# Filling the first image's idle matmul time, splitting weight stores over two queues, and pruning by weight rows: a convolution and attention kernel

## The chip, the cores and the metric

The kernel runs on one core of a Trainium2 chip. The metric is the device time of one execution, in microseconds (us). Five engines work beside each other, each in its own order: TensorE (PE in the profile, with its weight loads as PEld) multiplies matrices, VectorE (DVE) and ScalarE (ACT) work on tiles elementwise and reduce them, GpSimd (POOL) does some elementwise work, and SyncE (SP) starts DMA transfers. ScalarE can start transfers too. Engines wait for each other through semaphores. Matmul results arrive in PSUM and are read from there by VectorE or ScalarE.

## The reference, cut to what matters

Eight images of 512 channels and 32 x 32 pixels, in float32. Layer 0 is a residual block of a 1x1 convolution, two blocks of 3x3 convolution and attention, and a last 1x1 convolution over the four pieces; layer 1 is a depthwise and a pointwise convolution, with pruning of channels.

```python
# layer 0
t = cbs(x, cv1_w, cv1_bn, 0)              # cbs: convolution, batch norm, silu
ys = [t[:, :C], t[:, C:]]                 # C = 256
for i in range(2):
    yi = ys[-1]
    z = cbs(yi, m_cv1_w[i], m_cv1_bn[i], 1)            # 3x3
    z = bot_attention(z, m_qkv_w[i], m_rw[i], m_rh[i]) # 4 heads of 64, 1024 positions
    z = jax.nn.silu(bn_eval(conv2d(z, m_cv2_w[i], 0), m_cv2_bn[i]))
    ys.append(yi + z)
return cbs(jnp.concatenate(ys, axis=1), cv2_w, cv2_bn, 0)   # "the last convolution"

# layer 1
def _prune(x, thresh):
    amax = jnp.max(jnp.abs(x), axis=(2, 3), keepdims=True)
    return jnp.where(amax < thresh, jnp.zeros_like(x), x)
h = depthwise 3x3 of h, + dw_b
h = jax.nn.relu(_bn(h, ...))
h = _prune(h, 4.0)
h = pointwise 512 -> 512 of h, + pw_b
h = jax.nn.relu(_bn(h, ...))
h = _prune(h, 1e-3)

# both
x = x + layer0(_gn(x))     # _gn: group norm, 32 groups
x = x + layer1(_gn(x))
```

## The kernel before

Channels lie on the 128 partitions; an image is four tiles of 128 x 1024. Each engine keeps the order in which the program names its instructions (except GpSimd, which may be reordered), so this order decides what waits behind what. Background work is kept in lists of small functions that are "pumped" between others.

The 3x3 convolutions are computed in a transformed domain (a Winograd form). Their weights are transformed on the chip while the first image runs, written to DRAM (`u_dram`), and fetched from there for every image through a ring of four buffers. `along`, `inside` and `outside` are the steps for three pairs j of planes:

```python
    def transform_weights(l):
        ...
        def store(j, c, t):
            for m in range(2):
                src = t.rearrange("p (i m x) -> p i m x", i=2, m=2)[:, :, m]
                dst = u_dram[l][2 * j + m][:, :, c].rearrange("p i k o -> p i (k o)")
                nc.sync.dma_start(dst, src)
        def inner_rows(j, step): ...      # VectorE: "ucomp" tiles, stored
        def outer_rows(j, c, dy):         # ScalarE: "uplane" tiles, stored
            t = planes.pop((j, dy))
            nc.scalar.mul(t, t, 2.0)
            store(j, c, t)

    def ring_sources():                   # the order of all weight fetches
        for b in range(B):
            for l in range(2):
                for i in range(6):
                    yield u_dram[l][i]..., 2048
                yield wqkv[:, l]..., 1536
            for m in range(KC):
                yield w2[:, :, m * P : (m + 1) * P], 1024
    held = [len(sources) - 7, 0]          # fetches after these 7 are held until u1 is stored
```

The start of the program, for the first image:

```python
            fold = fold_norms()           # batch norm scales; GpSimd takes a power
            gn = [group_norm(pt, lambda c: pt[c], chunks) for chunks in ((0, 1), (2, 3))]
            ...
            pump(gn[1], 2)
            next(fold)
            flush(gn[1])
            next(fold)                    # waits for the power, then six small operations
            pump(first, 2)                # matmuls of the first convolution
            along, inside, outside = transform_weights(0)
            flush(along[0]); flush(along[2]); flush(inside[0]); flush(outside[0])
            ring_load(2)
            flush(first)
            flush(along[1]); flush(inside[1]); flush(outside[1])
            ring_load(2)
            flush(inside[2])
            pump(y0_work, 2)
            flush(outside[2])
            flush(y0_work)
            conv3(0, [], 0, [])
            ...
            qkv(0, ...)
            attention(taps, range(1, 20), lambda: None, [then])
            load(pt, 1)
```

The attention's end. `tail` is work for TensorE while the sums of the softmax are inverted, spread by DMA and multiplied into z; with `lambda: None` there is none:

```python
        parts, spread, check = sums(1)    # ps_dn on TensorE; ScalarE reads, VectorE inverts
        for part in parts:
            part()
        spread()                          # DMA: rw <- r
        tail()
        scale(1, 0)                       # VectorE: z = z * rw
        scale(1, 1)
        check()                           # ScalarE
```

What follows for every image (`halves` and `finishes` are work left from the image before, so they are empty in the first):

```python
        pump(finishes)
        cv2m(0)                           # ps_m: needs z
        pump(halves)
        conv3(1, halves, 1, finishes)     # ps_c: needs VectorE's transform of yp
        ...
        qkv(1, [], (0,) * 7)
        products, finish = cv2()          # the last convolution
        attention(stats[:KC], (6, 10, 14, 17), lambda: products(0, range(6)))
        stats = stats[KC:]
        cv2m(1)
        ...
        products(1, (0, 1, 2, 3))
        pump(stats)
        products(1, (4, 5))
        pump(stats)
        products(0, (6, 7))
        finish(0)                         # silu, then added to xt[0]
        ...                               # products(1, (6, 7)), finish(1), statistics, ...
```

`products(m, ks)` does the matmuls of output chunk m for the input chunks ks (0 and 1 are y0, 2 and 3 the first block's input, 4 and 5 its output, 6 and 7 the second block's output), two matmuls of 512 columns for each. Group norm's small steps:

```python
        def deviations():
            pv = ...                      # TensorE: group variance
            nc.vector.tensor_scalar(rs, pv[:, :n], 1e-5, None, ALU.add)
            nc.gpsimd.tensor_tensor(rs, rs, mhalf[:, :n], ALU.pow)
            nc.vector.scalar_tensor_tensor(nb, gm, -1.0, rs, ALU.mult, ALU.mult)
        def apply(i, c):
            nc.scalar.activation(dst(c), src[c], AF.Identity, bias=nb[...], scale=rs[...])
```

In the last image nothing of a next image is there to fill TensorE, and layer 1 is done with an order of its own. `taps(n)` are n of the 32 steps of the depthwise convolution on VectorE (eight for each chunk), `part(k, ...)` the pointwise products of input chunk k, `close(m)` relu and `finish(m)`:

```python
        def prune(c):
            keep = small.tile([P, 1], ...)
            nc.vector.tensor_reduce(keep, ht[c], AX.X, ALU.max)
            nc.vector.tensor_scalar(keep, keep, 4.0, None, ALU.is_ge)
            if c == KC - 1 and len(groups) == KC:
                w = wpw_sb[:, c, :]
                nc.vector.tensor_scalar(w, w, keep, None, ALU.mult)
            else:
                nc.gpsimd.tensor_scalar(ht[c], ht[c], keep, 1.0, ALU.mult, ALU.mult)

        def finish(m):
            w = box.pop(m)
            nc.vector.tensor_reduce(keep, w, AX.X, ALU.max)
            nc.vector.tensor_scalar(keep, keep, 1e-3, None, ALU.is_ge)
            nc.vector.scalar_tensor_tensor(xt[m], w, keep, xt[m], ALU.mult, ALU.add)
            nc.sync.dma_start(out[b, m * P : (m + 1) * P, :], xt[m])
    ...
    taps(3); relu(2); taps(2); prune(2); taps(6)
    part(2, every)
    relu(3); prune(3)
    for m in range(KC):
        part(3, [(m, 0), (m, 1)])
        close(m)
```

Of the kernel before, what the change touches and what calls it, by code (L numbers as in the profile page):

```python
# [1 line left out]

# [59 lines left out]
def fast_kernel(  # L62
# [174 lines left out]
    def transform_weights(l):  # L237
# [26 lines left out]
        def store(j, c, t):  # L264

            for m in range(2):
                src = t.rearrange("p (i m x) -> p i m x", i=2, m=2)[:, :, m]
                dst = u_dram[l][2 * j + m][:, :, c].rearrange("p i k o -> p i (k o)")
                nc.sync.dma_start(dst, src)
# [16 lines left out]
        def outer_rows(j, c, dy):  # L286
            t = planes.pop((j, dy))
            nc.scalar.mul(t, t, 2.0)
            store(j, c, t)
# [11 lines left out]
    def ring_sources():  # L301
        for b in range(B):
            for l in range(2):
                for i in range(6):
                    yield u_dram[l][i].rearrange("p a b c d -> p (a b c d)"), 2048
                yield wqkv[:, l].rearrange("p k o -> p (k o)"), 1536
            for m in range(KC):
                yield w2[:, :, m * P : (m + 1) * P], 1024
# [4 lines left out]
    held = [len(sources) - 7, 0]  # L313
# [14 lines left out]
    class Weights:  # L328
# [5 lines left out]
        def __exit__(self, *_):  # L334
            ring_load()

    def group_norm(src, dst, chunks):
# [24 lines left out]
        def deviations():  # L362
# [4 lines left out]
            nc.vector.scalar_tensor_tensor(nb, gm, -1.0, rs, ALU.mult, ALU.mult)  # L367

        def apply(i, c):
            nc.scalar.activation(  # L370
# [8 lines left out]
    def layer1_front(groups):  # L379
# [27 lines left out]
        def prune(c):  # L407
# [3 lines left out]
            if c == KC - 1 and len(groups) == KC:  # L411

                w = wpw_sb[:, c, :]
                nc.vector.tensor_scalar(w, w, keep, None, ALU.mult)
            else:
                nc.gpsimd.tensor_scalar(ht[c], ht[c], keep, 1.0, ALU.mult, ALU.mult)  # L416

        if len(groups) == KC:
# [12 lines left out]
    def layer1_back(b):  # L431
# [18 lines left out]
        def finish(m):  # L450
            w = box.pop(m)
            keep = small.tile([P, 1], F32, tag="keep2", name="keep2")
            nc.vector.tensor_reduce(keep, w, AX.X, ALU.max)
            nc.vector.tensor_scalar(keep, keep, 1e-3, None, ALU.is_ge)
# [417 lines left out]
    def cv2():  # L872
# [10 lines left out]
        def products(m, ks, ns=range(2)):  # L883
            if m not in open_:
                open_[m] = big_tile("ps_cv2"), ring.pop(0)
            ps, wt = open_[m]
            w = wt[:, : 2 * KC * P].rearrange("p (k o) -> p k o", o=P)
            for k in ks:
                for n in ns:
                    nc.tensor.matmul(  # L890
                        ps[:, n, :],
                        w[:, k, :],
                        rhs(k, n),
                        start=(k == 0),
                        stop=(k == 2 * KC - 1),
                    )

        def finish(m, pieces=1):
            ps, _ = open_.pop(m)
            ring_load()  # L900
            t = work_tile("c2")
            n, r = HW // pieces, 4 // pieces
            for q in range(pieces):
                act(t[:, q * n : (q + 1) * n], flat(ps)[:, q * n : (q + 1) * n], AF.Silu, BN1 + m)

                o = xt[m].rearrange("p (h t r) -> p h t r", t=F // 4, r=4)
                i = t.rearrange("p (r h t) -> p h t r", h=F, t=F // 4)
                o, i = (a[:, :, :, q * r : (q + 1) * r] for a in (o, i))
                nc.vector.tensor_tensor(o, i, o, ALU.add)

        return products, finish


    QUIET = (5, 8, 11, 14, 17, 18, 24, 26, 27, 28, 29, 30)
    halves, finishes, taps, before, late = [], [], [], [], []
    for b in range(B):
        if b:
# [9 lines left out]
            pump(late)  # L927
            pump(before, 2)
# [5 lines left out]
        else:  # L934
# [10 lines left out]
            flush(gn[1])  # L945
            next(fold)
            pump(first, 2)
            along, inside, outside = transform_weights(0)
            flush(along[0])
# [7 lines left out]
            flush(outside[1])  # L957
            ring_load(2)
            flush(inside[2])
            pump(y0_work, 2)  # L960
            flush(outside[2])
# [4 lines left out]
            along, inside, outside = transform_weights(1)  # L966
# [9 lines left out]
            attention(taps, range(1, 20), lambda: None, [then])  # L976
# [4 lines left out]
        cv2m(0)  # L981
        pump(halves)
# [4 lines left out]
        products, finish = cv2()  # L987
        attention(stats[:KC], (6, 10, 14, 17), lambda: products(0, range(6)))
# [5 lines left out]
        products(1, (0, 1, 2, 3))  # L994
        pump(stats)
        products(1, (4, 5))
        pump(stats)
        products(0, (6, 7))
# [53 lines left out]
    taps(2)  # L1052
# [6 lines left out]
    pump(gn[1])  # L1059
    before(1)  # L1060
# [496 lines left out]
```

## Time and profile before

| | us |
|---|---|
| time, median of 3 runs | 2702.61 (2702.23 to 2703.11) |
| profiled span | 2700.4, mean granted TensorE clock 0.992 |
| TensorE matmuls busy | 2631.7 (97%) |
| VectorE busy | 1978.2 (73%) |
| ScalarE busy | 1139.0 (42%) |
| GpSimd busy | 158.1 (6%) |
| DMA | 219.75 MB, mean 81 GB/s |

The page gives each engine's busy time, then the span in 40 slices with a digit for the busy tenths of each. Of a group of instructions it gives source line, engine, operation, written tile `<-` read tiles, shape and count. Nearly all instructions have the same source line, because a helper (`InOrder`) records them, so they are told apart by their tiles: `ps_c` are the 3x3 convolution's products, `ps_qk` and `ps_v` those before attention, `ps_s`, `ps_av` and `ps_dn` scores, values and sums, `ps_m` the block's 1x1 convolution, `ps_cv` the products of the first and of the last convolution, `ps_y` the first convolution's other half (y0), `ps_pw` the pointwise convolution, `pm` and `pv` group means and variances. A float32 matmul shows as two records. `SPq` and `ACTq` are DMA starts on SyncE's and ScalarE's queues. "Idle before, releaser" at the end of a row tells how long the engine stood still before it, and what ended that.

### The profile page before, as it was taken

Reading aid. Unit: us, or ns where it says so; the run is one execution under the profiler, and the core shown is the slowest. Engines: PE = TensorE matmul, PEld = TensorE weight load, DVE = VectorE, ACT = ScalarE, POOL = GpSimd, SP = SyncE. Lnnn points to the kernel's source line nnn. Section 1 sums busy time; section 2 is a strip of 40 time slices with the busy share of each in tenths; the row PEclk is TensorE's granted clock in tenths of the full one; section 3 lists DMA queues with packets and bytes.
Section 4 is the critical chain, followed back from the end, with each engine's and each line's share of the span. In section 5 each row is a group of like instructions: output and inputs, shape, how many; then the busy total and the mean of one; then the engine's idle time right before and its main releaser. Section 6 shows DMA issues by size and latency. Waiting matters only on the chain.

```text
span 2700.4 us, 36176 instructions
## 1 busy us (share of the span) xinstructions
PE 2631.7 (97%) x14958; PEld 1421.8 (53%) x14958; DVE 1978.2 (73%) x2693; ACT 1139.0 (42%) x1403; POOL 158.1 (6%) x100
## 2 busy tenths in 40 slices
PE   7989999999999999999999999999999999999996
PEld 4445464644646446464464644655455554646442
DVE  7776588764887649867588666886578865888557
ACT  3534335353362523525245353443434444253532
POOL 1000001000100001000010000100001000010000
PEclk9989999999999999999999999999999999999998
DMA  7341131211304023130130301313022221213100
GB/s 282 139 167 63 47 129 46 91 61 57 137 25 134 19 70 122 31 129 25 63 137 24 129 17 62 137 35 118 17 90 110 72 81 48 99 39 98 55 16 33
DMA packets 87261, 219.75 MB, mean 81 GB/s; under 512 B 5808, under 2 KB 51120, under 8 KB 74544
## 3 DMA queue, kind: packets, MB, share of 16 engines
q1 hardware_dynamic: 86800, 217.08, 23.6%
q8 instruction: 120, 1.97, 0.3%
q14 instruction: 53, 0.43, 0.1%
q10 hardware_dynamic: 288, 0.27, 0.0%
HBM read 171.19 MB, written 29.36 MB: 74 GB/s over the span
## 4 chain that ended last, share of the span: by engine, by line
PE 86%; DVE 10%; ACT 1%; issue 1%; DMA 0%; POOL 0%; SPq 0%; POOLq 0%; ACTq 0%; DVEq 0%
PE ps_cv L41 19%; PE ps_av L41 16%; PE ps_s L41 16%; PE ps_c L41 11%; PE ps_pw L41 8%; PE ps_qk L41 5%; PE ps_m L41 4%; PE ps_y L41 4%; DVE ht L41 4%; PE ps_v L41 2%; DVE kr L41 2%; PE ps_dn L41 1%; DVE keep L41 1%; ACT qy L41 1%; DVE mid L41 1%
## 5 line engine op out<-in xcount | busy, mean ns | idle before, releaser
L41 ACT ACTIVATE e<-ps_s 128x1024 f32<-128x1024 f32 x512 | 524.0, 1024 | 278.0 <-PE ps_s L41 269.0
L41 PE MATMUL ps_s<-qy,kr 64*64 64x512 f32 x4096 | 568.8, 592 | 2.0 <-ACT e L41 0.6
L41 PE MATMUL ps_av<-e,vt 64*64 64x512 f32 x4096 | 568.0, 591 | 1.1 <-ACT part L41 1.1
L41 DVE TENSOR_TENSOR sum<-sum,e 128x1024 f32<-128x1024 f32 x384 | 472.6, 1231 | 80.4 <-ACT e L41 73.1
L41 PEld LDWEIGHTS ps_av<-e,vt 64*64 64x64 f32 x4096 | 220.0, 133 | 229.5 <-issue 152.2
L41 PEld LDWEIGHTS ps_s<-qy,kr 64*64 64x64 f32 x4096 | 204.6, 133 | 249.6 <-issue 140.5
L41 DVE SCALAR_TENSOR_TENSOR ht<-xn,v_sb,ht 128x961 f32<-128x961 f32 (+1 forms) x256 | 330.3, 1298 | 7.5 <-ACT ht L41 2.5
L41 PE MATMUL ps_pw<-ht,wpw_sb 128*128 128x512 f32 x512 | 228.0, 601 | 5.0 <-POOL ht L416 5.0
L41 PE MATMUL ps_cv<-yp,wring 128*128 128x512 f32 x512 | 229.8, 596 | 0.0
L41 PE MATMUL ps_qk<-z,wring 128*128 128x512 f32 x512 | 225.7, 593 | 2.2 <-ACT z L41 2.2
L41 DVE TENSOR_TENSOR sum<-e 128x1024 f32<-128x1024 f32 x64 | 78.3, 1223 | 169.9 <-ACT e L41 169.9
L41 PEld LDWEIGHTS ps_pw<-ht,wpw_sb 128*128 128x128 f32 x512 | 96.9, 192 | 128.2 <-issue 121.6
L41 PEld LDWEIGHTS ps_qk<-z,wring 128*128 128x128 f32 x512 | 96.8, 190 | 118.1 <-issue 111.5
L41 PEld LDWEIGHTS ps_cv<-yp,wring 128*128 128x128 f32 x512 | 95.9, 190 | 113.8 <-issue 113.8
L41 ACT ACTIVATE c<-ps_cv,bi,sc 128x1024 f32<-128x1024 f32 (+1 forms) x33 | 38.8, 1178 | 229.5 <-PE ps_cv L41 229.4
L41 PEld LDWEIGHTS ps_c<-kr,wring 128*128 128x128 f32 x1024 | 120.2, 197 | 16.4 <-DVE kr L41 11.4
L41 PE MATMUL ps_c<-kr,wring 128*128 128x128 f32 x1024 | 120.6, 280 | 8.1 <-DVE kr L41 8.1
L41 ACT COPY c<-ps_c 128x256 f32<-128x256 f32 x96 | 35.5, 369 | 218.4 <-PE ps_c L41 212.2
L711 POOL TENSOR_TENSOR kr<-kr,v_sb 128x1024 f32<-128x1024 f32 x32 | 69.4, 2174 | 976.9 <-DVE kr L41 910.1
L41 PE MATMUL ps_c<-qy,wring 128*128 128x128 f32 x1024 | 118.9, 277 | 5.9 <-DVE y L41 5.9
L41 PE MATMUL ps_v<-wring,z 128*128 128x256 f32 x512 | 114.3, 381 | 8.1 <-DVE kr L41 8.1
L41 PE MATMUL ps_m<-z,wm_sb 128*128 128x512 f32 x256 | 114.4, 600 | 7.3 <-DVE z L41 7.3
(130 smaller groups left out, 3071.2 us busy)
## 6 DMA issues: line engine op xcount, KB each, us to landing
wring<-u SPq DMA_DIRECT2D x96, 1024.0 KB, 4.8
pt<-in_x SPq DMA_DIRECT2D x32, 512.0 KB, 6.0
rw<-r SPq DMA_DIRECT2D x64, 256.0 KB, 3.5
wring<-in_w SPq DMA_DIRECT2D x32, 512.0 KB, 4.5
xt<-in_x SPq DMA_DIRECT2D x32, 512.0 KB, 6.1
out<-xt SPq DMA_DIRECT2D x32, 512.0 KB, 2.7
wring<-in_wqkv SPq DMA_DIRECT2D x16, 768.0 KB, 4.2
u<-ucomp SPq DMA_DIRECT2D x24, 256.0 KB, 3.1
```

The costliest lines, as they stand in the source:

```text
L41: made = method(*args, **kwargs)
L711: nc.gpsimd.tensor_tensor(kk, kk, row.to_broadcast(full), ALU.add)
```

## The change

Five things are changed.

1. In the first image the last convolution begins early: `partial(0, 4)` does four input chunks of its output chunk 0 as the tail of the first block's attention, and `partial(1, 3)` three chunks of output chunk 1 after `cv2m(0)`. Their sums are copied to `ht`, which lies idle then, and added when the chunk is closed. The two weight tiles are fetched for this once more. TensorE is to have work where it stood still.
2. The outer planes' stores of the first block's weights go through ScalarE's queue, and the second pair of fetches comes after the third pair's stores. The stores are no longer to stand before fetches in one queue.
3. The norm scales are completed after VectorE's first row transforms, and the multiply that gives `nb` moves from the end of `deviations` to the first `apply`, so that VectorE does not stand waiting for GpSimd.
4. In the last image all four prunes scale the rows of the pointwise weights instead of the activations, and whether a channel reaches the limit is found by ScalarE: a relu of the value minus the number just below the limit, summed along the row, is above zero. Two of the four last prunes do the same. VectorE is relieved of reductions, and GpSimd's pass drops out.
5. Some taps move by one place, in the last image and in each image's first convolution.

```diff
-    def transform_weights(l):
+    def transform_weights(l, outer_queue):
...
-        def store(j, c, t):
+        def store(j, c, t, queue=nc.sync):
...
-                nc.sync.dma_start(dst, src)
+                queue.dma_start(dst, src)
...
-            store(j, c, t)
+            store(j, c, t, outer_queue)        # in outer_rows
...
+                if b == l == 0:
+                    for m in range(2):
+                        yield w2[:, :, m * P : (m + 1) * P], 1024
...
-    held = [len(sources) - 7, 0]
+    held = [len(sources) - 9, 0]
...
+    def reaches(t, i):
+        keep = small.tile([P, 1], F32, tag="keep3", name="keep3")
+        nc.scalar.activation(
+            work_tile("over"), t, AF.Relu, bias=below[:, i : i + 1], accum_out=keep
+        )
+        nc.vector.tensor_scalar(keep, keep, 0.0, None, ALU.is_gt)
+        return keep
...
-            nc.vector.scalar_tensor_tensor(nb, gm, -1.0, rs, ALU.mult, ALU.mult)
         def apply(i, c):
+            if i == 0:
+                nc.vector.scalar_tensor_tensor(nb, gm, -1.0, rs, ALU.mult, ALU.mult)
...
         if len(groups) == KC:
+            def prune(c):
+                keep = reaches(ht[c], 0)
                 w = wpw_sb[:, c, :]
                 nc.vector.tensor_scalar(w, w, keep, None, ALU.mult)
...
+            if b == B - 1 and m % 2 == 0:      # in finish of layer 1
+                keep = reaches(w, 1)
+            else: ...                          # as before
...
+        def partial(m, n):
+            ps = big_tile("ps_cv2")
+            with Weights() as wt:
+                some(ps, wt, range(n), range(2), 0, n - 1)
+            nc.scalar.copy(ht[m], flat(ps))
+            begun[m] = n
...
         def finish(m, pieces=1):               # of the last convolution
...
+            if m in begun:
+                nc.vector.tensor_tensor(ht[m], flat(ps), ht[m], ALU.add)
+            src = ht[m] if m in begun else flat(ps)
...
             pump(late)
+            pump(taps)                         # first convolution of images 1 to 7
             pump(before, 2)
...
             flush(gn[1])
+            pump(first, 2)
+            along, inside, outside = transform_weights(0, nc.scalar)
+            flush(along[0])
             next(fold)
-            pump(first, 2)
-            along, inside, outside = transform_weights(0)
-            flush(along[0])
             flush(along[2])
...
+            pump(y0_work, 2)
+            flush(inside[2])
+            flush(outside[2])
             ring_load(2)
-            flush(inside[2])
-            pump(y0_work, 2)
-            flush(outside[2])
             flush(y0_work)
...
-            attention(taps, range(1, 20), lambda: None, [then])
+            products, finish, partial = cv2()
+            attention(taps, range(1, 20), lambda: partial(0, 4), [then])
...
         cv2m(0)
+        if b == 0:
+            partial(1, 3)
...
-        attention(stats[:KC], (6, 10, 14, 17), lambda: products(0, range(6)))
+        def beside():
+            products(0, range(6) if b else (4, 5))
+            if b == 0:
+                products(1, (3, 4, 5))
+        attention(stats[:KC], (6, 10, 14, 17), beside)
...
-        products(1, (0, 1, 2, 3))
+        if b:
+            products(1, (0, 1, 2, 3))
         pump(stats)
-        products(1, (4, 5))
+        if b:
+            products(1, (4, 5))
+        products(0, (6, 7))
         pump(stats)
-        products(0, (6, 7))
...
-    taps(3); relu(2); taps(2); prune(2); taps(6)       # last image, written on one line here
+    taps(4); relu(2); taps(2); prune(2); taps(6)
```

## The prediction

> **What bounds the kernel now.** I read the page first (busy shares, then the 40 slices), then the busy time of each engine in stretches of 27 us, then the waits of TensorE, then the timeline around each wait. The page:
>
> ```profile
> PE 2631.7 (97%) x14958; PEld 1421.8 (53%) x14958; DVE 1978.2 (73%) x2693; ACT 1139.0 (42%) x1403; POOL 158.1 (6%) x100
> ...
> PE   7989999999999999999999999999999999999996
> ```
>
> TensorE is busy 2631.7 of 2700.4 us. Its idle time, 69 us, is the ceiling of a change that takes no matmul away, and none is taken away here (a slower clock apart, see below). The slices put it in the first 80 us, near 175 us, and at the end. The stretches (us; then PE, PEld, DVE, ACT, POOL busy; granted clock; DMA share; GB/s):
>
> ```profile
> 0.00:27.00 27.00, 14.20 (x32) 7.24 (x33) 13.78 (x41) 9.14 (x11) 9.90 (x12) 1.00 0.76 301
> 27.00:54.00 27.00, 23.88 (x81) 13.50 (x80) 26.48 (x35) 13.42 (x18) 0.00 (x0) 0.94 0.77 256
> 54.00:81.00 27.00, 20.76 (x158) 19.32 (x157) 19.46 (x47) 3.33 (x8) 0.00 (x0) 0.87 0.79 299
> ...
> 162.00:189.00 27.00, 14.65 (x53) 7.53 (x46) 16.14 (x24) 6.73 (x12) 0.00 (x0) 0.75 0.32 98
> ...
> 297.00:324.00 27.00, 27.00 (x67) 12.22 (x66) 5.58 (x13) 4.33 (x6) 1.02 (x1) 1.00 0.08 19
> ...
> 2646.00:2673.00 27.00, 21.35 (x51) 9.15 (x50) 25.20 (x31) 8.60 (x8) 4.40 (x3) 0.96 0.00 0
> 2673.00:2700.00 27.00, 15.46 (x31) 6.25 (x29) 16.69 (x19) 6.90 (x9) 0.00 (x0) 0.75 0.21 81
> ```
>
> Opening (0 to 81): 22 us idle, VectorE full in the second stretch. End of the first block of the first image (162 to 189): 12.35 us idle. Last two stretches: 17 us idle, VectorE at 25 of 27 in the first of them. In between TensorE is full, as at 297 to 324, apart from some 0.5 us per attention. The timeline names each wait (start, length, engine, what, idle before and releaser):
>
> ```profile
> 20.76 0.18 DVE L41 TENSOR_TENSOR sc<-sc,v_sb 128x24 f32<-128x24 f32 x1 [4.28 <-POOL sc L181]
> ...
> 55.05 5.63 SPq L41 DMA_DIRECT2D u<-uplane  x4
> ...
> 65.04 0.98 SPq L41 DMA_DIRECT2D wring<-u  x2
> ...
> 70.00 8.86 PE L41 MATMUL ps_c<-qy,wring 128*128 128x128 f32 x64 [5.90 <-DVE y L41]
> ...
> 79.20 7.41 PE L41 MATMUL ps_qk<-z,wring 128*128 128x512 f32 x16 [0.34 <-ACT z L41]
> ```
>
> VectorE loses 4.3 us behind GpSimd's power of the norm scales. The last pair of products starts at 70.0, 5 us after its weights are fetched at 65.0, and that fetch stands behind stores of 5.6 us in SyncE's queue; VectorE's y, named as the releaser, ended at 69.9, so both were late. The other waits:
>
> ```profile
> 172.27 7.86 PE L41 MATMUL ps_m<-z,wm_sb 128*128 128x512 f32 x14 [7.30 <-DVE z L41]
> ...
> 185.18 9.29 PE L41 MATMUL ps_c<-kr,wring 128*128 128x128 f32 x64 [5.05 <-DVE kr L41]
> ```
>
> ```profile
> 2669.26 8.32 DVE L41 SCALAR_TENSOR_TENSOR ht<-xn,v_sb,ht 128x961 f32<-128x961 f32 x6
> 2669.55 1.92 POOL L416 TENSOR_SCALAR ht<-ht,keep 128x1024 f32<-128x1024 f32 x1 [7.79 <-DVE keep L41]
> 2671.51 16.94 PE L41 MATMUL ps_pw<-ht,wpw_sb 128*128 128x512 f32 x32 [4.99 <-POOL ht L416]
> ```
>
> The chain that ended last runs through VectorE's taps and reductions in this end.
>
> **What the skill says.** "DMA: Bandwidth & Descriptors", Issuing engines are not separate DMA queues: transfers begun by the scalar, sync and gpsimd engines run on the same 16 DMA engines; a second issuer saves only sequencer time. So the stores on ScalarE's queue can gain by order and issue, not by bandwidth. The trace agrees that issue is what they cost: four stores take SyncE 2.6 us at 30.07 (0.65 each). "TensorE: Matmul & The Clock Gate", What's actually happening: after an idle window of about 3.4 us the clock falls to half and needs such a window of work to come back. The trace agrees: after 164.97 TensorE is idle, the clock is 0.50 from 170 to 174, and a ps_c group of 64 records takes 9.29 us at 185.18 against 7.31 at 194.31. "ScalarE: Activation LUTs", What ACT_TABLE_LOAD costs: about 1283 ns a load; the trace has 1.28 us.
>
> **The change part by part.** A full matmul of 512 columns is two records; eight records take 3.43 us in the chain (2599.18), so one costs 0.857 us.
>
> *Opening.* (a) VectorE's first row transforms no longer wait for the power: they can start at about 15.6 instead of 21.65 (the second statistics come 0.7 to 0.9 us earlier as the multiply waiting for GpSimd at 11.48 moves behind the next statistics; the raw weights issued at 3.20, 4.67 and 5.04 land 10.0, 10.4 and 11.9 us later, before 17). The six small fold operations, 0.9 us, come after them. The inner rows then begin near 22.2 instead of 27.56: 5.3 us. VectorE is continuous from there to 69.9, so 5 us should last. TensorE can take only 3.0 us of that at 47.83, as its ps_y work fills it to about 44, but its later groups have slack. (b) With the last stores no longer between two fetches in one queue, the weights of the last pair are there before about 58; the 5.9 us wait goes. z then follows VectorE: y at 64.8, the two closings and z as now (z was ready 9.3 us after y with the wait in it, about 3.4 without): qk near 68.3 instead of 79.2, that is 10.9 us. (c) Against it: ScalarE now issues 12 stores, 0.65 us each, 7.8 us, between its activations. It is only 13.4 of 27 us busy there, but the last y0 evictions come near 45.5 and the small edge column of kr behind them: 0.5 to 1 us of TensorE. A gap of some 3.5 us before qk may bring half clock, at most 1.7 us. I take 9.5.
>
> *First image.* Moved: partial(0) with 8 matmuls, 6.9 us, into the wait of 7.3; partial(1) with 6, 5.1 us, into the wait of 5.05. Removed later: the second block's tail falls from 12 to 10 matmuls (8.6 us, still longer than the 8.3 us from sums to z), and 12 matmuls between the last ps_m and the closing go: 14 x 0.857 = 12.0 us taken from a stage where TensorE is full. The next convolution itself is not brought forward by the filling: it is VectorE's chain (its transform runs without a gap from 186.8 to 209). But the clock stays full: the four ps_m groups end near 178.3 instead of 180.2, so 1.7 us on that chain. Added: two copies on ScalarE (about 1.0 us; the one at z now stands ahead of the table load, at most 0.8 us), two VectorE adds of 1.2 us, two weight fetches of 512 KB, all beside TensorE. In the closing VectorE's add, sum, statistics chain for two chunks ends some 15.5 us after ps_m, where TensorE arrives at 15.6: no wait, but no slack. A longer gap before the second qk (1.86 now, some 3.5 then) may cost up to 1.7 us of clock. I take 12.5.
>
> *Last image.* VectorE loses six reductions (four prunes, two closings) of 1.21 us and gains three weight-row scalings of 0.49 (the row at 2680.39); the fourth was there. Before the last relu that is 3 x (1.21 - 0.49) = 2.2 us. TensorE no longer waits for the 1.92 us on GpSimd: the third quarter starts near 2667.9 instead of 2671.5. But the last quarter still needs the taps, relu, a ScalarE sum (1.24 plus a 0.2 read), the comparison and the 0.49: near 2678.9 against about 2681. In the closing, four times reduce, compare and add (2.65 us each, from 2684.83 to 2695.5) become alternating ScalarE sums and VectorE reductions: ScalarE's 4 x 1.45 + 2 x 1.4 and one last 2.6, about 11.2 us against 12.1. Sum 3; up to 1.7 is lost again if the longer gap before the last quarter halves the clock.
>
> *Images 2 to 7.* One tap earlier in the first convolution, and the small multiply of the norms later in VectorE's order: TensorE is full there, worth nothing either way.
>
> Sum: 9.5 + 12.5 + 3 = 25 us, so 2702.6 - 25 = 2677.6; I say 2678.
>
> **The rivals.** (1) The gap is filled but the work only moves: if the closing of the first image becomes VectorE-bound without its 12 filler matmuls, the 12 us come back as waits of the small means matmul. For it: my count has no slack (15.5 against 15.6). Against it: VectorE is only 5.6 of 27 busy at 297 to 324. Wholly true: about 2690. (2) ScalarE as DMA issuer becomes the opening's bound: its stores wait for work buffers' transfers in order, and the silus, edge columns and z behind them wait too. For it: SyncE's four stores took up to 5.6 us when they had to wait. Against it: ScalarE is half idle. It could take 5 to 8 us: 2684. (3) The last pair's fetch stays late because all the weights go out and come back through the same DMA engines (share 0.93 at 55 to 65): 2 to 4 us lost. (4) Better: in the opening the gaps keep full clock and the last image gains its whole 5: 2672.
>
> **Range and chances.** The three sums are independent; each may be off by 2 to 4 us, downward more likely, as waits moved tend to come back: 2671 to 2688. For 2% the time would have to reach 2648.6, which takes 54 of the 69 us of idle time: 0.01. For slower by 2%, 54 us would have to be added to an engine list that is nearly the same: 0.01. Within 2%: 0.98.
>
> **What would show it.** In the changed profile: no SCALAR_TENSOR_TENSOR or fold wait on GpSimd of 4 us on VectorE; qk at about 68 to 70; the 5.9 us wait gone; stores on ACTq at about 0.65 each; no wait over 1 us at ps_m near 160 and at the ps_c after it; the second image some 22 us earlier; TensorE still full in the closing of the first image; no wait for POOL ht at the end. Wrong if qk comes after 73, if pm waits over 2 us in the first image's closing, or if the middle images change in length.

## The result and the profile after

| | before | after |
|---|---|---|
| median of 6 runs, us | 2703.03 (2702.23 to 2704.61) | 2679.77 (2678.50 to 2682.62) |
| ratio | | 0.9915, 95% interval 0.9902 to 0.9928 |
| profiled span, us | 2700.4, granted clock 0.992 | 2680.8, granted clock 0.995 |

The change saves 23 us. The page of the changed kernel, the same two lines as were read before: the matmuls need as long as they did (2629.3 us against 2631.7), and the third and the last slice have filled by one step each.

```profile
PE 2629.3 (98%) x14958; PEld 1416.4 (53%) x14958; DVE 1955.8 (73%) x2692; ACT 1152.6 (43%) x1417; POOL 162.5 (6%) x99
...
PE   7999999999999999999999999999999999999997
```

The stretches of 27 us (PE, PEld, DVE, ACT, POOL busy; granted clock; DMA share; GB/s):

```profile
27.00:54.00 27.00, 23.77 (x87) 14.26 (x86) 22.66 (x33) 11.43 (x16) 0.00 (x0) 0.94 1.02 352
54.00:81.00 27.00, 24.67 (x167) 19.80 (x166) 25.23 (x53) 6.05 (x11) 0.93 (x1) 1.00 0.60 221
162.00:189.00 27.00, 26.02 (x138) 17.60 (x137) 20.35 (x37) 8.96 (x18) 0.00 (x0) 1.00 0.70 253
297.00:324.00 27.00, 26.58 (x68) 12.02 (x67) 12.65 (x26) 11.75 (x9) 1.72 (x2) 1.00 0.28 106
2626.00:2653.00 27.00, 23.45 (x60) 10.54 (x59) 23.41 (x33) 11.08 (x12) 2.90 (x2) 1.00 0.00 1
```

At 54 to 81 TensorE gained 3.9 us of busy time at a higher clock; at 162 to 189 its idle time fell from 12.35 to 1 us and the clock rose from 0.75 to 1.00. The closing of the first image (297 to 324) stays full to 0.42 us. TensorE's stretch from 27 to 54 is as before (23.77 us busy against 23.88), and the timeline of the opening says why (ACTq: stores issued by ScalarE):

```profile
15.25 0.68 DVE L43 TENSOR_TENSOR wtmp<-qy 128x512 f32<-128x512 f32 x1
...
36.20 2.37 ACTq L43 DMA_DIRECT2D u<-uplane  x2
...
43.84 1.06 ACT L43 ACTIVATE uplane<-uplane 128x1024 f32<-128x1024 f32 x1 [2.83 <-DMA u<-ucomp]
...
47.10 1.45 ACT L43 ACTIVATE y<-ps_y,bi,sc 128x512 f32<-128x512 f32 x2 [2.21 <-DMA u<-ucomp]
48.44 0.22 ACT L43 ACTIVATE kr<-v 128x32 f32<-128x32 f32 x1
...
48.71 7.25 PE L43 MATMUL ps_c<-kr,wring 128*128 128x128 f32 x48 [3.23 <-ACT kr L43]
```

VectorE starts its transforms at 15.25, as it should. But each pair of stores on ScalarE's queue holds ScalarE for 1.19 to 2.37 us. Its two idle times of 2.83 and 2.21 us, which the profile puts down to the transfer of earlier stores, each hold such a pair as well (1.83 us from 41.96 and 1.21 us from 45.84). So the edge column of kr, 0.22 us of work, comes at 48.44, and TensorE waits 3.23 us for it. The 48 products behind that gap took 7.25 us, which is as long as 64 take later: the granted clock is 0.5 from 48.74 to 52.16, which is called half clock from here on. How long this wait is differs between profiles: in b_open, h_fill, i_tail, k_warm and l_idle below, which have the same opening, it is 1.56 to 3.51 us, and the first q and k start at 70.37 to 72.60.

The first image:

```profile
164.75 6.28 PE L43 MATMUL ps_m<-z,wm_sb 128*128 128x512 f32 x14 [0.30 <-DVE z L43]
...
176.12 7.38 PE L43 MATMUL ps_c<-kr,wring 128*128 128x128 f32 x64
...
201.52 8.83 PE L43 MATMUL ps_qk<-z,wring 128*128 128x512 f32 x16 [2.14 <-ACT z L43]
...
315.00 0.38 PE L43 MATMUL pm<-mv,g_sb 128*128 128x2 f32 x2 [0.42 <-DVE nb L43]
```

The waits of 7.30 and 5.05 us are 0.30 and none, and `ps_c` runs at full clock (7.38 instead of 9.29). Behind the gap of 2.14 us, however, q and k took 8.83 us, where the kernel before took 7.41 at full clock behind its gap of 1.86. In the last image the two last quarters of the pointwise products:

```profile
2651.63 7.10 PE L43 MATMUL ps_pw<-ht,wpw_sb 128*128 128x512 f32 x16 [3.48 <-DVE wpw_sb L43]
...
2662.39 8.80 PE L43 MATMUL ps_pw<-ht,wpw_sb 128*128 128x512 f32 x16 [3.65 <-DVE wpw_sb L43]
```

GpSimd is gone from this wait; VectorE's weight rows are what TensorE waits for, and the last quarter ran in part at half clock.

Start of the same work in both profiles, and what each part gained:

```
                              before     after   earlier by   in this part
first q and k (opening)        79.20     71.69       7.5          7.5
second image's ps_y           367.54    348.53      19.0         11.5
last image's first pm        2611.35   2593.48      17.9         -1.1
end                          2700.4    2680.8       19.6          1.7
```

The profiled execution was the slowest of the six (2682.62), so its 19.6 us are less than the medians' 23.

One thing that the diff held and neither the account of the change nor the prediction mentions: where the last convolution's chunk is closed in one piece, ScalarE's silu now reads PSUM in permuted order and writes in pixel order, so that VectorE's addition to xt reads in order, in every image. The costliest groups, before, then after, show it (operation, shapes, count; busy us, mean ns):

```profile
L41 DVE TENSOR_TENSOR xt<-c,xt 128x1024 f32<-128x1024 f32 x31 | 61.0, 1968 | 39.6 <-ACT c L41 39.6
```

```profile
L43 ACT ACTIVATE c<-ps_cv,bi,sc 128x1024 f32<-128x1024 f32 x29 | 34.9, 1204 | 168.7 <-PE ps_cv L43 168.6
L43 ACT ACTIVATE c<-ht,bi,sc 128x1024 f32<-128x1024 f32 x2 | 4.4, 2178 | 8.3 <-DVE ht L43 8.3
...
L43 DVE TENSOR_TENSOR xt<-c,xt 128x1024 f32<-128x1024 f32 x31 | 37.9, 1224 | 28.3 <-ACT c L43 28.2
```

VectorE saves 0.74 us on each of 31 additions. ScalarE pays nothing for it from PSUM (1204 ns before too), but 2178 ns for the two chunks that it reads from `ht` in SBUF.

### The profile page after: what moved, and what is told of

Same layout as the page of the kernel before. It is cut to its first block, busy times and chain, and to the rows that moved or that the text cites. A ratio compares the mean times of both kernels' runs of the same rounds, so it can differ in the third digit from the quotient of the medians.

```text
span 2680.8 us, 36189 instructions
## 1 busy us (share of the span) xinstructions
PE 2629.3 (98%) x14958; PEld 1416.4 (53%) x14958; DVE 1955.8 (73%) x2692; ACT 1152.6 (43%) x1417; POOL 162.5 (6%) x99
## 3 DMA queue, kind: packets, MB, share of 16 engines
q10 hardware_dynamic: 3552, 3.41, 0.4%
## 4 chain that ended last, share of the span: by engine, by line
PE 90%; DVE 5%; ACT 2%; DMA 1%; issue 1%; POOL 0%; SPq 0%; ACTq 0%; POOLq 0%; DVEq 0%
PE ps_cv L43 19%; PE ps_av L43 16%; PE ps_s L43 16%; PE ps_c L43 11%; PE ps_pw L43 7%; PE ps_qk L43 7%; PE ps_v L43 4%; PE ps_m L43 4%; PE ps_y L43 4%; DVE kr L43 1%; PE ps_dn L43 1%; DVE ht L43 1%; ACT qy L43 1%; DVE mid L43 1%; DMA u<-ucomp 0%
## 5 line engine op out<-in xcount | busy, mean ns | idle before, releaser
L43 ACT ACTIVATE e<-ps_s 128x1024 f32<-128x1024 f32 x512 | 524.1, 1024 | 281.0 <-PE ps_s L43 271.5
L43 DVE SCALAR_TENSOR_TENSOR ht<-xn,v_sb,ht 128x961 f32<-128x961 f32 (+1 forms) x256 | 335.9, 1318 | 25.0 <-ACT ht L43 19.9
L43 DVE TENSOR_TENSOR sum<-e 128x1024 f32<-128x1024 f32 x64 | 78.4, 1224 | 174.8 <-ACT e L43 173.8
L43 DVE RECIPROCAL r<-ps_dn 128x128 f32<-128x128 f32 x128 | 114.7, 927 | 6.9 <-ACT r L43 6.9
L43 PE MATMUL ps_c<-vt,wring 128*128 128x128 f32 x1024 | 117.2, 275 | 0.7 <-ACT c L43 0.7
```

Of the source, the lines that this page charges most:

```text
L43: made = method(*args, **kwargs)
```

## The experiments

The theory: the three parts are independent and add; what is missing from the predicted 25 us was lost to ScalarE's stores and to stretches of half clock behind the gaps that are left. The rivals: the work only moves (the closing of the first image gets it back), or the stores and fetches set the opening whatever queue they are in.

### One part at a time

Each of these is the kernel before with one part of the change. First image only (part 1 of the list, with the old closing of a chunk, so that little else differs; the last products of chunk 0 also stand one place earlier in every image):

> The kernel before with the first image's part alone: partial(0, 4), partial(1, 3) and what they take away later; the silu of the last convolution written as before. Theory (14 matmuls leave a stage where TensorE is full, plus the clock that stays full, less one half-clock stretch at the second qk): the distance from the first scores of the first image to the second image's first mean shortens by 11 to 12 us, total about 2691.5. Rival (the work only moves, the closing becomes VectorE-bound): under 4 us, about 2699 or more.

```diff
+ attention(..., lambda: partial(0, 4), ...)   + partial(1, 3)   + beside()
  all else as before
```

Measured: 2692.00 us (2691.04 to 2693.64) against 2703.19, ratio 0.9958 (0.9942 to 0.9975): 11.2 us. In the profile the image is 10.6 us shorter between first q and k and the second image. This rules out that the work only moved, which would have given 2699 us or more.

Opening only (parts 2 and 3, also with the old closing of a chunk):

> The kernel before with the opening's part alone: ScalarE's queue for the outer stores, the later second pair of fetches, the norm scales after the first row transforms, nb at the first apply. Theory: the first qk starts at about 71.7 as in the changed kernel, 7.5 us earlier than before, and all of it reaches the end: about 2695.5. Rival: the opening's gain is partly taken back in the first block's attention, whose weight stores start earlier: under 5 us at the end.

```diff
+ transform_weights(0, nc.scalar)   + ring_load(2) after outside[2]   + next(fold) after along[0]   + nb in apply
  all else as before
```

Measured: 2696.65 us (2692.64 to 2698.83), ratio 0.9974 (0.9965 to 0.9983): 6.5 us. The first q and k start at 71.75, as in the full change. But the second ones are only 4.4 us earlier: in this profile the first block had a wait that neither before nor after shows at that length,

```profile
128.96 1.09 PE L43 MATMUL ps_s<-qy,kr 64*64 64x512 f32 x8 [2.70 <-ACT e L43]
```

and more half clock behind its long waits, which are still there (17.1 us between 162 and 186, against 13.7 between 168 and 190 before).

Last image only (part 4 and the last image's share of parts 3 and 5, old closing of a chunk), and the new closing of a chunk alone:

> The kernel before with the last image's part alone (prunes by ScalarE sums and weight rows, nb behind a tap, the moved taps), the silu of the last convolution written as before. Theory A (pruning is what shortened the last image): 1.5 to 2 us, about 2701. Theory B (the other form of the silu, which makes VectorE's add read contiguously, carried it): 0 to 0.5 us, about 2702.5.

> The kernel before with one thing changed: ScalarE's silu of the last convolution reads its sums in the permuted order and writes in pixel order, so VectorE's add into xt reads contiguously. The add falls from 1.95 to 1.23 us in both theories. Theory A: it is off the path in the full images and worth under 0.7 us in the last. Theory B: three such adds lie on VectorE's chain in the last image, so about 2 us: 2700.5.

```diff
 c_last: + reaches(), prune by weight rows, moved taps; all else as before
 f_form: + silu from PSUM in permuted order; all else as before
```

Measured: 2701.30 us (2697.77 to 2704.44), ratio 0.9993 (0.9986 to 1.0000), and 2701.72 us (2700.60 to 2703.18), ratio 0.9994 (0.9985 to 1.0003). 1.9 and 1.5 us against ranges of 6.7 and 2.6 us: small. f_form's interval includes no difference at all, and c_last's ends at none, so neither is clear of no difference. The four medians' sum, 11.2 + 6.5 + 1.9 + 1.5 = 21.1 us, is near the 23.3 of the whole, so the parts add to within the spread. None of the four holds the taps that were moved in the first convolution of images 2 to 8; no run tests those alone. With the opening code as before, a_first, c_last and f_form name the last pair's fetch as what TensorE waits for; a_first's waits (us in total, times, longest):

```profile
PE ps_c L43 <- DMA wring<-u: 6.0, 1, 6.0
```

So in these three the weights come last. In the kernel before, the profile named VectorE's y, which ended 0.1 us before the wait did: there both were late.

### The opening: is it ScalarE's queue?

The outer stores back on SyncE's queue, the later fetches kept:

> The changed kernel with the outer planes' stores back on SyncE's queue, the later place of the second pair of fetches kept. Theory A (the second queue brought the weights in time): the waits for wring come back, qk at 74 or later, total 2682 or more. Theory B (the order of fetches brought them in time, and the second queue only holds up ScalarE): ScalarE's edge column is there early, qk at 69 to 71, total 2677 to 2679.

```diff
-            along, inside, outside = transform_weights(0, nc.scalar)
+            along, inside, outside = transform_weights(0, nc.sync)
```

Measured: 2684.09 us (2682.19 to 2684.36), 4.3 above the change. The edge columns come at 45.38 instead of 48.44, but the weights are late:

```profile
55.44 10.00 PE L43 MATMUL ps_c<-vt,wring 128*128 128x128 f32 x64 [3.63 <-DMA wring<-u]
...
73.80 1.55 PE L43 MATMUL ps_qk<-z,wring 128*128 128x512 f32 x3 [1.21 <-ACT z L43]
```

q and k start 2.1 us later. The second queue is worth that at this point, its price on ScalarE paid.

The other way round: the stores stay with ScalarE, and VectorE takes the edge columns from it:

> The changed kernel, but in the first image's first 3x3 convolution the six edge columns (128 x 32 each) are written by VectorE and not by ScalarE. Theory A (TensorE's 3.2 us wait at the first ps_c comes from the edge column standing behind ScalarE's stores and their waits): the wait falls under 0.7 us, the first qk comes at 69 to 69.5 instead of 71.7, total 2677 or a little more. Theory B (VectorE's chain is the bound of the opening anyway): six more operations of some 0.2 us on it, qk at 71.7 to 73, total 2680 to 2681.

```diff
-            nc.scalar.mul(o[0][:, :, 0], x[:, :, 0, 1], -1.0)
+            nc.vector.tensor_scalar(o[0][:, :, 0], x[:, :, 0, 1], -1.0, None, ALU.mult)   # first image, first block
-            nc.scalar.copy(o[3][:, :, last], x[:, :, last, 0])
+            nc.vector.tensor_copy(o[3][:, :, last], x[:, :, last, 0])
```

Measured: 2679.72 us (2679.34 to 2681.38): nothing gained. The timeline of TensorE:

```profile
43.48 7.31 PE L43 MATMUL ps_c<-kr,wring 128*128 128x128 f32 x64
...
54.11 9.01 PE L43 MATMUL ps_c<-vt,wring 128*128 128x128 f32 x64 [3.32 <-DVE mid L43]
...
71.44 3.75 PE L43 MATMUL ps_qk<-z,wring 128*128 128x512 f32 x8 [1.17 <-ACT z L43]
```

The wait for kr is gone, and a wait for VectorE of the same length stands one pair later. The third pair starts at 62.95 in both kernels: the second pair started 1.7 us earlier than in the change (54.11 against 55.80) and took 1.7 longer (9.01 against 7.31). So the clock was the next suspect. Three matmuls whose result nobody reads go into that gap:

> The changed kernel with the edge columns on VectorE and three matmuls whose result nobody reads in the gap of 3.3 us between the first and the second pair of products of the opening. Theory (of the 2 us by which the opening missed its 9.5 some 1.7 are the half clock behind this gap, 9.0 against 7.3 us for the second pair): first q and k at 69.7 instead of 71.4, total 2678. Rival (VectorE's closings or the weights set the pace of the third pair anyway): q and k at 71.4, total 2679.7.

```diff
+    def idle(n):
+        t = bank_tile("idle")
+        for _ in range(n):
+            nc.tensor.matmul(t, w1_sb[:, 0, :P], y0[:, 0, :512], start=True, stop=True)
...
         rows_back(products(0), inner_planes[1][:, :512])
+        idle(3)                                    # with the edge columns on VectorE
```

```profile
53.55 7.38 PE L43 MATMUL ps_c<-vt,wring 128*128 128x128 f32 x64 [0.55 <-DVE mid L43]
60.77 7.31 PE L43 MATMUL ps_c<-qy,wring 128*128 128x128 f32 x64
69.26 6.98 PE L43 MATMUL ps_qk<-z,wring 128*128 128x512 f32 x15 [1.18 <-ACT z L43]
```

Measured: 2678.31 us (2676.15 to 2679.98), and q and k at 69.26, 2.2 us earlier than without the three matmuls; m_all below, with the same opening, has them at 69.24. That is 9.9 us before the old start: the predicted 9.5 and a little more. The second pair keeps full clock. i_tail, with the opening of the change, happened to have no half clock in it either, and a wait for kr of 1.56 us; its q and k start at 70.37. The medians of n_open and d_edges lie 1.4 us apart, with ranges that overlap.

### The first image: what is the closing's slack, and what the clock?

Four more real matmuls (two input chunks of output chunk 2, whose weights are fetched once more) in the gap before the second q and k:

> The changed kernel with four more matmuls begun early in the first image: two input chunks of output chunk 2 between the second block's ps_c and qk, into the wait of 2.1 us. Theory A (the gap halved the clock of qk, which took 8.8 us instead of 7.4): qk starts 1.3 us later but runs at full clock, so attention starts within 0.3 us of where it did, and 3.4 us of work leave the closing: total 2676.4. Theory B (the clock does not depend on this gap): attention starts 1.3 us later, total 2677.7.

```diff
-        conv3(1, halves, 1, finishes)
+        conv3(1, halves if b else [lambda: partial_banks(2, 2)], 1 if b else 0, finishes)
```

Measured: 2682.12 us (2680.98 to 2685.41), a loss of 2.4. TensorE's timeline in that kernel:

```profile
203.38 7.03 PE L43 MATMUL ps_qk<-z,wring 128*128 128x512 f32 x16
...
315.04 0.59 PE L43 MATMUL pm<-mv,g_sb 128*128 128x2 f32 x2 [3.82 <-DVE nb L43]
315.49 3.76 PE L43 MATMUL ps_cv<-yp,wring 128*128 128x512 f32 x4
319.04 4.51 PE L43 MATMUL ps_cv<-qy,wring 128*128 128x512 f32 x8
```

q and k run at full clock, 7.03, but the closing now waits 3.82 us for the means' chain on VectorE. In the changed kernel that wait is 0.42; the four matmuls taken away are 4 x 0.857 = 3.43, and 0.42 + 3.43 = 3.85. So the closing has no slack, as the prediction counted, and the matmuls moved out of it beyond this point came back as a wait, with half clock behind it (3.76 and 4.51 us for 4 and 8 records, where 1.96 and 3.60 are full clock). The rival "the work only moves" is wrong for the change, and right for the next four matmuls beyond it.

Two idle matmuls in the same gap instead, which take nothing from the closing:

> The changed kernel with two matmuls whose result nobody reads in the gap of 2.1 us before the second block's q and k in the first image. Theory (the half clock after that gap is the 1 us by which the first image missed its 12.5): q and k take 7.0 instead of 8.83 us, every later milestone is 1.8 us earlier, total 2678. Rival (the time comes back in the closing, which has no slack, as it did when real matmuls were moved): second image no earlier than now, total 2680.

```diff
-        conv3(1, halves, 1, finishes)
+        conv3(1, halves if b else [lambda: idle(2)], 1 if b else 0, finishes)
```

Measured: 2677.41 us (2675.78 to 2678.42), 2.4 below the change; q and k take 7.41 us, and the second image starts 2.1 us earlier (346.44), 0.4 of it from the opening. Not all of the 2.4 need come from this gap, since the last image had less half clock in this run too (the table below). And k_warm, the kernel of the section on the last image, has nothing in this gap and shows 7.40 in its profile, behind the same 2.14 us:

```profile
201.89 7.40 PE L43 MATMUL ps_qk<-z,wring 128*128 128x512 f32 x16 [2.14 <-ACT z L43]
```

So the length of the gap alone does not decide; the granted clock in that stretch, of the change first and then of k_warm, shows the difference (columns as above, the clock third from the end):

```profile
201.50:205.00 3.50, 3.48 (x5) 1.50 (x6) 2.10 (x5) 1.29 (x2) 0.00 (x0) 0.62 1.02 341
```

```profile
201.50:205.00 3.50, 3.11 (x7) 1.36 (x8) 2.10 (x5) 1.29 (x3) 0.00 (x0) 1.00 1.02 336
```

In every trace the stretches of half clock within the work last 3.41 us, or two or three times that, and within one trace they lie on one grid of 3.41 us, whose pieces are called steps here: in the change they begin at 48.74, 202.34, 2618.98 and 2663.35 us, which are 45, 708 and 13 steps of 3.413 us apart. One step at half clock costs up to 1.7 us where TensorE is busy.

How a gap lies to the grid decides. In the change the step before 202.34 holds the whole gap (TensorE is idle for 2.14 us of it), and the next step is at half clock. In k_warm the grid cuts the same gap at 200.41, into 0.66 and 1.48 us, and no half clock follows. Cut into steps in this way from 15 us on, the 14 traces agree: each full-clock step with 2.0 us or more of idle TensorE is followed by half clock, none with 1.85 us or less is, and between 1.87 and 1.96 both occur (the ends of matmuls are modelled, so these limits are estimates from the traces). The grid lies differently in each run, so the same code gets half clock in one run and not in the next. The Trainium skill has this in "TensorE: Matmul & The Clock Gate", What's actually happening: a free-running activity window of 3413 ns, and therefore counts that vary between runs. The traces agree. They do not agree with what the prediction took from there, that the clock falls after an idle window of about 3.4 us: here some 2 us of idle time within one step were enough.

### The last image

The tap that stands before `nb` (it was to hide GpSimd's power) moved behind it again:

> The changed kernel with the tap in the last image's norm put behind nb again, so that VectorE stands still while GpSimd takes the power. Theory A (a tap beside it stretches GpSimd's power from 0.56 to about 1.5 us, so the tap hides little): the power takes 0.56 us again, VectorE's chain is longer by only 3 x 0.25 = 0.7 us, total 2680.5. Theory B (GpSimd's time there has another cause): the power stays at 1.4 to 1.5 us, and the chain is longer by 3 x 1.25 us: 2683.5.

```diff
-    taps(1)
     before(c)            # c = 1, 2, 3
+    taps(1)
```

Measured: 2681.05 us (2679.08 to 2683.84): no gain over the change, and no loss that the spread would show. The power and VectorE around it, in the changed kernel and then in this one:

```profile
2609.02 1.25 DVE L43 SCALAR_TENSOR_TENSOR ht<-xn,v_sb,ht 128x992 f32<-128x992 f32 x1
2609.13 1.55 POOL L386 TENSOR_TENSOR rs<-rs,mhalf 128x1 f32<-128x1 f32 x1 [12.60 <-DVE rs L43]
2610.72 0.16 DVE L43 SCALAR_TENSOR_TENSOR nb<-gm,rs 128x1 f32<-128x1 f32 x1 [0.45 <-POOL rs L386]
```

```profile
2607.47 0.56 POOL L386 TENSOR_TENSOR rs<-rs,mhalf 128x1 f32<-128x1 f32 x1 [12.60 <-DVE rs L43]
2608.07 0.16 DVE L43 SCALAR_TENSOR_TENSOR nb<-gm,rs 128x1 f32<-128x1 f32 x1 [0.67 <-POOL rs L386]
```

Beside the tap the power takes 1.55 us instead of 0.56; it ends 0.4 us after the tap does, so it seems to do its work only then. All three powers behind a tap are long in the change (1.42 to 1.55 us) and short in i_tail (0.55 to 0.56). The Trainium skill states the reason in "SBUF — State Buffer", SBUF: two separate sides: a VectorE operation with two SBUF inputs and a GpSimd operation that reads SBUF exclude each other for a whole instruction. The trace agrees, and of the wait of 0.67 the tap hides 0.22, not all.

The clock in this image: three matmuls with zero weights, which add nothing to the sums, in each of the two gaps before the last two quarters:

> The changed kernel with three matmuls with zero weights (they add nothing to the sums) in each of the two gaps before the third and the last quarter of the last image's final convolution. Theory (the gaps of 3.5 us, not the work, put one of the quarters at half clock: 8.80 against 7.10 us): both quarters take 7.1 us, and the last stretch, from its first means matmul to the end, falls from 87.3 to about 85.6 us; total 2678. Rival (the sums and adds behind the last quarter set the end whatever the clock): stretch unchanged at 87.3, total 2680.

```diff
+    pad(1)               # 3 matmuls, zero weights, into banks already begun
     part(2, every)
+    pad(2)
     relu(3)
```

```profile
2655.40 2.74 PE L43 MATMUL ps_pw<-ht,zero 128*128 128x512 f32 x6
2659.22 7.11 PE L43 MATMUL ps_pw<-ht,wpw_sb 128*128 128x512 f32 x16 [1.08 <-DVE wpw_sb L43]
```

Measured: 2678.34 us (2676.43 to 2679.74), 1.4 below the change with overlapping ranges. The last quarter takes 7.11 instead of 8.80, and the last stretch (from the first pm of the last image to the end) 84.7 us instead of 87.3. Most of that is not the padding: across kernels that have the same code up to that quarter, apart from the padding, its start depends on the half clock that an earlier gap in the last image happened to get (times from that first pm; half clock between 20 and 40 us after it, in steps of 3.41 us):

```
            half clock in 20 to 40   last quarter starts   takes   last stretch
change              6.8 us                68.91             8.80       87.3
e_sync              6.8                   69.11             8.80       87.6
n_open              6.8                   69.01             8.80       87.4
d_edges             3.4                   67.63             7.10       85.2
m_all               3.4                   67.64             7.10       85.2
h_fill              3.4                   67.63             8.80       86.2
l_idle              0.0                   66.88             7.10       84.5
k_warm              0.0                   66.89             7.11       84.7
```

With the same half clock before it, the padded and the unpadded kernel have the same last stretch: m_all and d_edges 85.2, k_warm 84.7 and l_idle 84.5. What half clock in the last quarter itself costs is seen in h_fill against d_edges: 86.2 against 85.2. Both padded kernels have that quarter at full clock, and so have two of the six without padding. That the padding shortens the time is therefore not shown; it leaves gaps of at most 1.08 us there, too short to bring half clock by the count above. Nor does half clock cost time at every place: in l_idle the quarter before took 8.71 us,

```profile
2647.50 8.71 PE L43 MATMUL ps_pw<-ht,wpw_sb 128*128 128x512 f32 x16 [3.29 <-DVE wpw_sb L43]
2658.26 7.10 PE L43 MATMUL ps_pw<-ht,wpw_sb 128*128 128x512 f32 x16 [2.04 <-DVE wpw_sb L43]
```

and its end came no later, because TensorE waited for VectorE behind it all the same.

### All together

> The three fillings and the edge columns on VectorE together. Theory, if the parts add: 0.3 + 1.7 + 1.8 + 1.7 = 5.5 us less than the changed kernel, 2674 to 2675. Rival (each is given back at the next wait): 2679 to 2680.

The edge columns on VectorE, `idle(3)`, `idle(2)` and both `pad`s: 2675.83 us (2675.54 to 2676.28), ratio to before 0.9900 (0.9884 to 0.9917). It is the fastest version, and its slowest run lies below the fastest of the change. By the medians it gains 3.9 us of the expected 5.5; the parts alone (n_open, l_idle, k_warm: 1.5, 2.4 and 1.4) add to 5.3. The profile of this run has no half clock in the first 330 us; one step of it is left under the work of the last image, from 2615.33. It is also the most even version: its four runs lie within 0.7 us, the six of the change within 4.1. The six runs of the change, by their mean granted clock, show that the 4.1 go with the clock:

```
clock 0.995: 2682.62  2682.01
clock 0.996: 2679.96  2679.57
clock 0.997: 2678.50  2678.66
```

## Why the prediction was right, point by point

*The total.* 2678 was said, 2679.8 came, inside the range of 2671 to 2688, and a gain of 25 us was counted where 23.3 came. "Within 2%" came, for the reason given: only idle time of TensorE could be won.

*Opening, 9.5.* It was 7.5 in the profile, so q and k at 71.69 missed the announced 68 to 70. The mechanism was right in (a) and (b): VectorE starts at 15.25 (said: 15.6), and the wait for the last pair's weights is gone. The term that failed is (c), the price of ScalarE as issuer: 0.5 to 1 us of TensorE was said, and it was a wait of 3.23 us, with half clock behind it. Of rival (2), "its stores wait ... and the silus, edge columns and z behind them wait too", this much came true. d_edges shows that a second wait of the same length lay hidden behind it, for VectorE, which the prediction did not have: with the first one gone, q and k still came at 71.44. n_open shows that 9.9 us were there once the clock is kept: what was missing was lost at the gap, not at the stores' bandwidth. Rival (3), a fetch that stays late, is what e_sync brings back (3.63 us at the second pair) and the second queue all but prevents: of the kernels with it, i_tail alone shows such a wait, 1.30 us.

*First image, 12.5.* It was 11.5 here, with a half-clock step in q and k, which the prediction allowed for ("up to 1.7 us"), though it expected a gap of 3.5 us there and 2.14 came. In k_warm, with the same code in this image and without that step, the same part is 12.6 us shorter than before (288.3 to 275.8). The term held, the slack too: 15.5 against 15.6 was counted, a wait of 0.42 us came, and h_fill showed that there was nothing beyond. The prediction's own test, "wrong if pm waits over 2 us in the first image's closing", was not met by the change, but was by h_fill.

*Last image, 3, less up to 1.7 for the clock.* It was 1.7, with the last quarter at half clock. In l_idle and k_warm the last stretch is 84.5 and 84.7 us, against 89.1 before, which had 10.2 us of half clock under its work. What the term would be with the clock equal on both sides is not shown. The wait for GpSimd is gone, as was said. Two things were not counted. The moved tap stands beside GpSimd's power and hides a third of the wait for it. And the cheaper addition of the last convolution, 0.74 us an instance on VectorE, was overlooked; how much of the last image's gain is its, the runs do not separate (c_last and f_form are each hardly clear of the spread).

*Images 2 to 7, nothing.* From the second image's ps_y to the last image's first pm the change takes 2244.95 us against 2243.81, 1.1 us more. Taken strictly, this is one of the prediction's signs of being wrong ("if the middle images change in length"). But the kernels with the same code in these images differ by 0.8 us among themselves (e_sync 2244.18, h_fill 2244.98), and a_first and f_form, which lack the moved tap, are 0.9 and 0.3 above the kernel before. So the tap is not needed for it; the cause stays open.

*The size of the spread.* The prediction took the clock as a cost that a gap may bring. The runs showed that for each gap of some 2 us or more it depends on where the grid happens to lie, at up to 1.7 us for each step of half clock, and that the times of the change's six runs go with their clocks.

## What to carry to other kernels

Count a gap of TensorE at its length plus up to 1.7 us for each step of half clock that may follow. Where it cannot be filled with useful work, try idle matmuls in it: in the opening and before the second q and k they kept the clock here and cost nothing that was seen. Before work is moved out of a full stage into a gap, count the slack of the stage it leaves; when it was used up here, the four matmuls moved came back as a wait of their own length. An engine that issues transfers between its other work delays small pieces of that work which others wait for: look for the smallest tile behind the issue, here an edge column of 0.22 us for which TensorE waited 3.23. Look then for the wait behind it too: with this one gone, d_edges was no faster.

## What the runs showed of the hardware that was not expected

- Half clock comes in steps of 3.41 us on a grid that differs from run to run: the same code behind the same gap of 2.14 us took 8.83 us in one profile and 7.40 in another. A step with 2.0 us or more of idle TensorE was followed by half clock in every trace, from 15 us on.
- A power of 128 x 1 on GpSimd took 1.55 us beside a VectorE tap with two SBUF inputs, and 0.56 alone.
- ScalarE reads a permuted 128 x 1024 tile from PSUM in 1204 ns, as fast as in order, but takes 2178 ns for the same order from SBUF (two instances); VectorE's addition took 1968 ns with its permuted operands and 1224 in order.
- Two stores issued by ScalarE held its queue for 1.19 to 2.37 us in the opening of the change.
